# Folding the first four tiles' rows four items earlier, in the last group of the down stage

## The chip, the cores and the metric

The kernel runs on one core of a Trainium2 chip. The time is device microseconds (us) of one execution, the median of several. The core has five engines: TensorE (PE in the profile, its weight loads PEld), VectorE (DVE), ScalarE (ACT), GpSimd (POOL), and SyncE (SP), which here only issues DMAs. ACT can issue DMAs as well, and the kernel uses that in one place.

## The reference, cut to what matters

There are 2 x 1024 = 2048 rows of width 1024. A first part with a sparse gate is followed by a layernorm, then a feed-forward network with 2-rank LoRA terms and a second layernorm.

```
s = silu(x @ w_gate.T)                       # 2752 wide
s[the k = 1376 smallest of |s| in each row] = 0
s = s * (x @ w_up.T)
x = layernorm(x + s @ w_down.T)

def qlora(x, wq, A, B):                      # A: 2 x d, B: h x 2
    return x @ tile(wq, (1, 4)).T + (x @ A.T @ B.T) * 0.5
gate = silu(qlora(x, w1q, a1, b1))
up = qlora(x, w3q, a3, b3)
x = layernorm(x + qlora(gate * up, w2q, a2, b2))
```

`tile(wq, (1, 4))` repeats a weight of width 256 four times, so `x @ tile(wq).T` equals the sum of the four 256-wide quarters of a row times `wq`. The kernel calls that sum the fold. The products `x @ A.T` are four dot products of length 1024 for each row (two of a1, two of a3).

## The kernel before, in words

The rows are cut into 16 tiles of 128 and these into 4 groups of GT = 4 tiles. All matrix products use fp32 values split into two parts of a shorter form, high and low (names ending in h and l), so that each product is done in three passes: high by high, high by low, low by high. The stages follow each other: gate and up for all groups, the selection of the largest values (DVE and ACT), then `down` for the groups 0 to 3, then `ffn` for the groups 0 to 3.

**`down(g)`** has six blocks of the 2752-wide inner dimension (512, 512, 512, 384, 384, 448) times the 4 tiles of the group: 24 items. An item loads its values m and its mask u on SP's queue (L710, L711), makes the mask a number on ACT (L724), multiplies on POOL (L725), transposes on PE (L745, L747) into PSUM, copies the high part on ACT (L749) and the low part on DVE (L750), then multiplies with the weights on PE (L765), and DVE adds the result to `acc` (L768). After the last block of a tile follow its layernorm (L568 and on, with a power on POOL in L580 and an application on ACT in L588) and a store of the row tile to `x_d` in DRAM (L787). Weights for a block come either from a stored split (L684) or raw (L603), and then ACT makes the high part (L173) and POOL the low part (L174).

**The last group of down** does the beginning of the ffn beside its items. From the fifth item on, `ffn_consts` is advanced by one step for each item: four loads of the rows of a1 and a3 to all partitions, `abc` (L798), and then for each of 8 blocks of the hidden width the matrix `br` of the LoRA factors b1 and b3: a memset (L806), six small loads (L810), a split on ACT and POOL (L173, L174), and two DMAs on ACT's queue (L813). Their staging buffers `braw` have two copies. From the item on at which the block number is `f1` = 2, `f1_first` is advanced by one step for each item. For t = 0 to 3 it loads tile 8 + t (L656), makes the four dot products of that tile on DVE (L659), then the fold and the LoRA factors of tile t (`f1_tile`), and, one step later, their transposes (`f1_tile2`).

**`f1_tile(t)`** loads the tile of x (`x2a`, L920, 512 KB), adds the quarters in three operations on POOL (L927, L928, L929) into `fold`, and lays the four dot products out in `tl` (a memset on POOL, L933, and small operations on DVE, L931 to L940). **`f1_tile2(t)`** does four transposes on PE (L949, L951), a copy of the high part on ACT (L954) and of the low part on DVE (L955). The dot products of the tiles 0 to 7 are made earlier in `down`. `fold` and `tl` have one buffer each, `x2a` two, and `fh` and `fl`, the copies' results, six. In `f1_first` the dot products' throwaway output also goes to the buffer `fold` of that step.

**`ffn(g)`** has 8 blocks x 4 tiles: 14 matmuls each (L981 to L984), a silu on ACT (L987), and products on DVE (L988, L990), with further work on ACT (L992) and POOL (L994). Beside the blocks 0, 2, 4 and 6 it makes the folds of the next group's tiles (tiles 4 to 7 in group 0), by the same two functions. After that come `f2` and the second layernorm.

**The order.** The order of the instructions of each engine is fixed when the kernel is built, by a scheduler which plans with its own model of time from the order in which the program issues them. SP's DMA queue is in program order as the scheduler left it.

Of the kernel before, what the change touches and what calls it, by code (L numbers as in the profile page):

```python
# [32 lines left out]
GT = 4  # L33
# [19 lines left out]
class Ring:  # L53
    def __init__(self, n, slots, dt):
        self.n, self.slots, self.dt = n, slots, dt
# [10 lines left out]
class Kern:  # L66
    def __init__(self, tc, A, O):
        self.tc, self.nc, self.A, self.O = tc, tc.nc, A, O
        self.nt = A["xt"].shape[0]
        self.x_seen = False  # L70
        self.lasta = self.lastv = self.lastd = None
        self.pend = self.lastp = None
        self.cache, self.wd_d, self.wd_g, self.wst = {}, {}, {}, []

# [533 lines left out]
    def down(self, g, f1=None, early=0):  # L608
        n, ea = 0, []
        for ib in range(len(DB)):  # L610
            if f1 is not None:
                if ib == f1:
                    self.fg = self.f1_first()
            ws = []
            for t in range(g * GT, (g + 1) * GT):
                st = {"e": n} if n < early else {}
                load = lambda: self.down_load(st, ib, t, n)
                prep = lambda st=st, ib=ib: self.down_prep(st, ib)
                mm = lambda st=st, ib=ib, t=t, ws=ws: self.down_mm(st, ib, t, ws)
                if n < early:  # L620
                    load()
                    ea.append((self.pend, prep))
                    self.q2.append(mm)
                    if n == early - 1:
                        for j in range(2):
                            yield
                            with self.behind():
                                for e in ea:
                                    e[j]()
                        self.pend = None  # L630
                        yield
                else:
                    self.masks()
                    self.item(lambda: (load(), self.down_w(g, ib, ws)), prep, mm, 2, 3)
                n += 1
                if g == 0 and n == 12:
                    self.tkg = self.topk(self.nt // GT - 1, 2)
                if (n > 11 or g) and self.tkg and next(self.tkg, 1):
                    self.tkg, self.dg = None, self.dots_down()
                if f1 is not None and n > 4:  # L640
                    next(self.fcg, None)
                    if ib >= f1:
                        next(self.fg, None)
                for _ in range(2 if n % 2 else 1):
                    next(self.dg, None)
        if f1 is not None:
            list(self.fg)
            self.masks()
        yield

    def f1_first(self):
        for t in range(GT):
            f, x2 = self.f1_room()
            jk, o = f.bitcast(U8), t + 2 * GT
            with self.load_behind():
                self.nc.sync.dma_start(x2, self.x_d[o])  # L656
            for i in range(4):
                with self.behind():
                    self.nc.vector.scalar_tensor_tensor(  # L659
                        jk, x2, 0.5, self.abc[:, i, :], ALU.mult, ALU.mult, accum_out=self.dall[:, o, i : i + 1]  # L660
                    )
                if i < 3:
                    yield
            self.f1_tile(t, f)
            yield
            self.f1_tile2(t)

    def f1_room(self):
        return (self.fp.tile([P, w], F, tag=n, bufs=b, name=n) for n, w, b in (("fold", 2 * P, 1), ("x2a", H, 2)))
# [119 lines left out]
    def ffn_consts(self):  # L789
        nc, fp = self.nc, self.fp  # L790
        A = self.A
        self.br = fp.tile([P, NI], R, name="br")
        self.abc = fp.tile([P, 4, H], F, name="abc")
        self.fst, self.c2 = {}, False
        for i in range(4):
            yield
            with self.load_behind():
                nc.sync.dma_start(  # L798
                    self.abc[:, i, :], A[("a1", "a3")[i // 2]][i % 2 : i % 2 + 1, :].partition_broadcast(P)
                )  # L800
        for b in range(NB):
            yield
            bs = slice(b * BW, (b + 1) * BW)
            sv = fp.tile([P, 2, BW], F, tag="sv", bufs=2, name="braw")
            raw, lo = sv[:, 0], sv[:, 1].bitcast(R)
            nc.gpsimd.memset(raw, 0.0)  # L806
            with self.load_behind():
                for w, n in ((0, "b1t"), (32, "b3t")):
                    for i in range(3):
                        nc.sync.dma_start(raw[w + 2 * i : w + 2 * i + 2, :], A[n][:, bs])  # L810
            self.split(self.br[:, bs], lo, raw)
            for w in (0, 32):
                nc.scalar.dma_start(self.br[w + 2 : w + 4, bs].bitcast(F), lo[w + 2 : w + 4, :].bitcast(F))  # L813
# [278 lines left out]
```

## Time and profile before

| quantity | value |
|---|---|
| median of 3 runs | 1924.16 us (1921.65 to 1924.33) |
| the profiled execution | 1926.91 us |
| its span | 1925.1 us |
| mean granted TensorE clock | 0.993 |
| PE busy | 1885.3 us, 98% of the span |
| DVE, ACT, POOL busy | 64%, 47%, 51% |
| DMA, mean over the span | 254 GB/s |

The page's rows of groups give, for each line and engine, the operation, its buffers and shapes, how often it ran, its busy time and mean, and the idle time just before it with what ended it. In the timeline each row is the start in us from the span's start, the busy time, the engine and line, the operation and, in square brackets, the idle time before and its releaser. A duration of a PE row overlaps with the next row's start, so the pace is read from one start to the next. The last group of down lies, on PE, at about 1330 to 1475 us; the first blocks of ffn follow.

### The profile page before, as it was taken

Reading aid. Unit: us, or ns where it says so; the run is one execution under the profiler, and the core shown is the slowest. Engines: PE = TensorE matmul, PEld = TensorE weight load, DVE = VectorE, ACT = ScalarE, POOL = GpSimd, SP = SyncE. Lnnn points to the kernel's source line nnn. Section 1 sums busy time; section 2 is a strip of 40 time slices with the busy share of each in tenths; the row PEclk is TensorE's granted clock in tenths of the full one; section 3 lists DMA queues with packets and bytes.
Section 4 is the critical chain, followed back from the end, with each engine's and each line's share of the span. In section 5 each row is a group of like instructions: output and inputs, shape, how many; then the busy total and the mean of one; then the engine's idle time right before and its main releaser. Section 6 shows DMA issues by size and latency. Waiting matters only on the chain. (4 is left out here: it accounts for less than half of the span.)

```text
span 1925.1 us, 29381 instructions
## 1 busy us (share of the span) xinstructions
PE 1885.3 (98%) x10825; PEld 1754.4 (91%) x10825; DVE 1229.6 (64%) x1831; ACT 904.0 (47%) x1448; POOL 973.0 (51%) x606
## 2 busy tenths in 40 slices
PE   9999999999999999999999999999998999998998
PEld 9999999999999999999888787888787979898896
DVE  4633556767358574691238998688467857779565
ACT  4333477414883258622246533323333746557362
POOL 5655664445445354355565443554565746436062
PEclk9999999999999999999999999999999999999999
DMA  7677687676977868667798756977776878485651
GB/s 266 237 250 260 236 325 261 210 272 253 330 231 241 314 235 303 236 228 256 282 328 285 270 188 227 337 245 261 268 250 244 279 284 321 155 318 177 229 196 66
DMA packets 166205, 488.66 MB, mean 254 GB/s; under 512 B 24772, under 2 KB 45380, under 8 KB 166056
## 3 DMA queue, kind: packets, MB, share of 16 engines
q1 hardware_dynamic: 165848, 486.43, 71.9%
q8 instruction: 85, 1.39, 0.3%
q14 instruction: 64, 0.52, 0.1%
q10 hardware_dynamic: 208, 0.31, 0.0%
HBM read 370.30 MB, written 116.33 MB: 253 GB/s over the span
## 5 line engine op out<-in xcount | busy, mean ns | idle before, releaser
L174 POOL TENSOR_TENSOR wl<-wr,wh 128x1376 fp32r<-128x1376 f32 (+2 forms) x187 | 566.4, 3035 | 466.1 <-ACT wh L173 436.8
L353 PE MATMUL mm<-wh,xh 128*128 128x344 f32 x1928 | 610.4, 322 | 2.8 <-DMA wh<-tw3T1h 2.8
L353 PE MATMUL mm<-wh,xl 128*128 128x344 f32 x1928 | 609.8, 320 | 0.0
L173 ACT CAST wh<-wr 128x1376 fp32r<-128x1376 f32 (+2 forms) x192 | 232.4, 1215 | 340.9 <-PE mm L353 199.6
L353 PEld LDWEIGHTS mm<-wh,xh 128*128 128x128 f32 x1928 | 364.7, 189 | 3.0 <-issue 3.0
L353 PEld LDWEIGHTS mm<-wh,xl 128*128 128x128 f32 x1928 | 364.6, 189 | 0.0
L353 PE MATMUL mm<-wl,xh 128*128 128x344 f32 x1928 | 342.1, 319 | 0.0
L353 PEld LDWEIGHTS mm<-wl,xh 128*128 128x128 f32 x1928 | 310.1, 188 | 0.0
L765 PE MATMUL mm<-wh,mh 128*128 128x512 f32 x680 | 217.8, 400 | 0.1
L765 PE MATMUL mm<-wl,mh 128*128 128x512 f32 x680 | 215.1, 395 | 1.1 <-POOL wl L174 1.1
L765 PE MATMUL mm<-wh,ml 128*128 128x512 f32 x648 | 205.5, 396 | 0.8 <-DVE ml L750 0.8
L460 ACT ACTIVATE jk<-a,cur 128x2752 int8<-128x2752 f32 x66 | 170.8, 2588 | 31.2 <-DVE cur L482 15.8
L994 POOL TENSOR_TENSOR hf<-hf,gt 128x344 f32<-128x344 f32 x96 | 142.2, 1491 | 75.6 <-DVE gt L988 68.7
L725 POOL TENSOR_TENSOR m<-m,ub 128x512 f32<-128x512 f32 (+2 forms) x93 | 111.0, 1194 | 128.0 <-ACT ub L724 65.8
L981 PE MATMUL mm<-wh,fh 128*128 128x344 f32 x512 | 166.2, 325 | 5.8 <-DVE gt L988 5.2
L983 PE MATMUL mm<-wh,fl 128*128 128x344 f32 x512 | 164.0, 320 | 0.0
L982 PE MATMUL mm<-wl,fh 128*128 128x344 f32 x512 | 163.9, 320 | 0.0
L765 PEld LDWEIGHTS mm<-wl,mh 128*128 128x128 f32 x680 | 127.4, 188 | 30.1 <-POOL wl L174 2.2
L768 DVE TENSOR_TENSOR acc<-acc,mm 128x1024 f32<-128x1024 f32 x96 | 116.4, 1214 | 57.9 <-PE mm L765 27.8
L765 PEld LDWEIGHTS mm<-wh,mh 128*128 128x128 f32 x680 | 124.7, 189 | 24.8 <-ACT mh L749 0.5
L765 PEld LDWEIGHTS mm<-wh,ml 128*128 128x128 f32 x648 | 121.2, 189 | 26.9 <-DVE ml L750 1.0
L992 ACT ACTIVATE pa<-pa 128x344 f32<-128x344 f32 x256 | 123.0, 483 | 38.6 <-DVE pa L990 34.0
(191 smaller groups left out, 2742.5 us busy)
## 6 DMA issues: line engine op xcount, KB each, us to landing
wr<-wu SPq DMA_DIRECT2D x64, 688.0 KB
wr<-wg SPq DMA_DIRECT2D x52, 688.0 KB
wr<-wd SPq DMA_DIRECT2D x48, 512.0 KB
s_d<-cc SPq DMA_DIRECT2D x64, 344.0 KB
m_d<-mt SPq DMA_DIRECT2D x64, 344.0 KB
a<-s_d SPq DMA_DIRECT2D x64, 344.0 KB
wl<-wc_w SPq DMA_DIRECT2D x48, 344.0 KB
wh<-wc_w SPq DMA_DIRECT2D x48, 344.0 KB
```

The costliest lines, as they stand in the source:

```text
L173: self.lasta = self.nc.scalar.copy(hi, raw)
L174: (eng or self.nc.gpsimd).tensor_tensor(lo, raw, hi.bitcast(F), ALU.subtract)
L353: self.nc.tensor.matmul(o, l, r, start=start and n < m and n % (2 * KH) == 0, stop=stop and n >= m and (n - m) % KH == KH - 1)
L460: nc.scalar.activation(jk.bitcast(I8), av[j], AF.Sign, bias=t, scale=-1.0, accum_out=s)
L725: nc.gpsimd.tensor_tensor(m[:, :w], m[:, :w], ub[:, :w], ALU.mult)
L765: nc.tensor.matmul(ps[:, h], a, b[:, h * 512 : (h + 1) * 512], start=i == 0, stop=i == len(ops) - 1)
L768: nc.vector.tensor_tensor(out, out, ps.rearrange("p a b -> p (a b)"), ALU.add)
L981: nc.tensor.matmul(o, fh[:, c, :], wh[:, c, :], start=c == 0, stop=False)
L982: nc.tensor.matmul(o, fh[:, c, :], wl[:, c, :], start=False, stop=False)
L983: nc.tensor.matmul(o, fl[:, c, :], wh[:, c, :], start=False, stop=False)
L992: nc.scalar.activation(pa[:, r], pa[:, r], AF.Copy, scale=0.5, accum_out=part[:, r, b : b + 1])
L994: G.tensor_tensor(hf[:, hs], hf[:, hs], gt, ALU.add)
```

## The change

The first tile's fold, `f1_tile(0)`, is called once when block `f1` − 1 = 1 begins, ahead of `f1_first`. In `f1_first`, step t now begins with the transposes of tile t (`f1_tile2(t)`), then loads tile 8 + t and makes its dot products, and then calls `f1_tile(t + 1)`, the fold of the next tile. So tile 0's fold is made eight items sooner, those of tiles 1 to 3 and all four tiles' transposes four items sooner. Two assignments move to the constructor. The number of instructions on each engine does not change.

```diff
@@ __init__
         self.lasta = self.lastv = self.lastd = None
+        self.fst, self.c2 = {}, False
...
@@ down
             if f1 is not None:
+                if ib == f1 - 1:
+                    self.f1_tile(0)
                 if ib == f1:
                     self.fg = self.f1_first()
...
@@ f1_first
         for t in range(GT):
+            self.f1_tile2(t)
             f, x2 = self.f1_room()
...
                 if i < 3:
                     yield
-            self.f1_tile(t, f)
-            yield
-            self.f1_tile2(t)
+            if t < GT - 1:
+                self.f1_tile(t + 1, f)
+                yield
...
@@ ffn_consts
         self.abc = fp.tile([P, 4, H], F, name="abc")
-        self.fst, self.c2 = {}, False
```

## The prediction

> **What bounds the kernel now.** I read the page's first part, then the waits of PE in the stretch that the change touches (1330 to 1560 us of the span), then PE's timeline there.
>
> ```profile
> PE 1885.3 (98%) x10825; PEld 1754.4 (91%) x10825; DVE 1229.6 (64%) x1831; ACT 904.0 (47%) x1448; POOL 973.0 (51%) x606
> ```
>
> PE is the bound nearly everywhere. The change leaves every engine's instruction count alone, so it can only move PE's waits and the slow-clock stretches behind them. The waits of PE by releaser (total us, times, longest):
>
> ```profile
> PE tp L949 <- POOL fold L929: 3.2, 2, 1.9
> ...
> PE tp L745 <- POOL m L725: 1.6, 1, 1.6
> ...
> PE tp L745 <- DVE fl L955: 1.2, 1, 1.2
> PE mm L765 <- POOL wl L174: 1.1, 3, 0.5
> PE mm L765 <- DVE ml L750: 0.8, 1, 0.8
> PE mm L981 <- DVE hf L988: 0.5, 1, 0.5
> PE tp L951 <- DVE tl L940: 0.4, 1, 0.4
> ```
>
> These sum to 8.8 us (the L1028 and three L988 rows lie after 1525 us and are not touched). PE's timeline places them:
>
> ```profile
> 1376.14 0.66 PE L745 MATMUL tp<-ident,m 128*128 128x128 f32 x4 [1.62 <-POOL m L725]
> ...
> 1381.59 0.44 PE L949 MATMUL tp<-ident,fold 128*128 128x128 f32 x2 [1.35 <-POOL fold L929]
> ...
> 1457.91 0.55 PE L745 MATMUL tp<-ident,m 128*128 128x128 f32 x3 [1.17 <-DVE fl L955]
> ...
> 1477.96 0.44 PE L949 MATMUL tp<-ident,fold 128*128 128x128 f32 x2
> 1478.78 0.41 PE L951 MATMUL tp<-ident,tl 128*128 128x128 f32 x2 [0.38 <-DVE tl L940]
> 1481.06 0.44 PE L949 MATMUL tp<-ident,fold 128*128 128x128 f32 x2 [1.87 <-POOL fold L929]
> ```
>
> Two of the places also cost clock. In the windows (length, PE busy, granted clock, DMA share, GB/s):
>
> ```profile
> 1461.00:1463.00 2.00, 2.00 (x6) 0.56 0.77 295
> 1479.00:1481.00 2.00, 0.19 (x2) 1.00 0.91 264
> 1483.00:1485.00 2.00, 2.00 (x9) 0.56 0.96 391
> ```
>
> Behind 1459.3 eight down matmuls take 3.5 us where they take 1.84 at full clock (.461 a pair): 1.7 lost. Behind 1483.2 twelve of the ffn take .287 each instead of .157: 1.5 lost. The waits at 1376 and 1381 lose none. The whole reachable loss is 8.8 + 1.7 + 1.5 = 12.0 us, against a profiled execution of 1926.91 (span 1925.1, 1.8 around it), itself 2.75 above the median of 1924.16. No gain can pass 12 us; I apply differences to the median.
>
> **The change part by part.** F0 to F7 are the transposes L949/L951 of tiles 0 to 7, T1 to T96 the item transposes L745. In the built order PE has 2,080 down matmuls L765. Before, F0 to F4 stand after 1752, 1848, 1944, 2026 and 2058 of them; after, F0 to F3 after 1656, 1778, 1854 and 1960.
>
> 1. Tile 0's fold, eight items sooner. The L920 load (512 KB) goes on SP's queue right behind a store L787 at about 1330 (before: 1351.4), ahead of the next k_d and abc loads, each pushed by one issue, .3 to .7 us. A load of that kind issued at 1349.2 landed at 1357.7 with the DMA share at 1.03; at 1330 the share is .99, so 5 to 8 us, landing 1335 to 1338. The fold is three POOL operations at .74 to 1.37 (2.5 in the 1478 row), now ahead of the last layernorm's L580 and one mask L725. Of the next item's prep, the first need, PE has some 3 us in hand; if the load lands after 1338, each us costs one. I take 0, bounds 0 and 3. F0 at about 1354 finds its fold some ten us old: the 1.35 wait goes. Gain 1.35.
>
> 2. T82's wait of 1.62. Its cause is ACT:
> ```profile
> 1372.26 0.59 ACT L749 CAST mh<-tp 128x512 fp32r<-128x512 f32 x1 [6.39 <-DMA br<-braw]
> ```
> The L813 pair on ACT's queue holds ACT for 6.4 us, so the mask cast L724 and L725 are late. After, 20 down matmuls (4.6 us) more stand ahead of T82, but POOL has tile 1's fold (2.5) ahead of that mask. 4.6 − 2.5 leaves 2.1 against a wait of 1.62. Gain 1.6, bounds 0 and 1.6. F1 has then 26 more matmuls behind T82's place to wait in; its fold is about 3 us ahead. No wait.
>
> 3. F3 and the item behind it. Before, F3's copy L954 stands behind two casts that wait for a weight load:
> ```profile
> 1453.09 1.44 ACT L173 CAST wh<-wr 128x688 fp32r<-128x688 f32 x2 [7.76 <-DMA wr<-w]
> 1454.43 0.58 ACT L954 CAST fh<-tp 128x512 fp32r<-128x512 f32 x1
> ```
> fl, T94 and the next ml follow late: 1.17 + .77, and 1.7 of half clock. After, F3 stands 66 matmuls (15 us) earlier and its copy behind only the first cast; T94 and T95 have 75 straight matmuls behind them. Gain 3.6, bounds 1.5 (the cast still late) and 3.6.
>
> 4. New ACT order. The casts L724 of items 17 and 18 (before at 1402.1 and 1407.9) and F2's copy now stand behind an L813 pair that waits for its split; T88, T89, T90 and F3 hang on them. The row nearest is again an L813 hold, 6.39 here and 5.78 at 1418; against it stand 3 to 4 us by which masks and copies run ahead of PE. If the pair issues with the gap of the single row (.57 to 2.3), it costs nothing; with one full hold 2 to 3; with both more (rival B). I take 1.0, between, nearer the small end since only one braw of two is still in flight.
>
> 5. Weight splits L174 on POOL. Folds stand ahead of two of them: 2.5 us of delay for a wl that now is .27 to .5 late in three places (1.1 in all). Bounds 0.4 and 4; I take 1.5, so 0.4 worse.
>
> 6. F4 to F7. Before, F4 stands at the end of down, F5 after 2 blocks of ffn work (14 matmuls each, 2.2 us), F6 and F7 side by side after 3: the .38 and 1.87 waits and the 1.5 of clock. Cause: there is one fold buffer, and the next fold starts only when its reader is done. L949 to L949 is 3.1 us (1477.96 to 1481.06). After, F4 and F5 stand side by side after 3 blocks, F6 after 6, F7 after 10. So the pair still exists, for other tiles: wait 3.1 − .44 = 2.7, in place of .38 + 1.87 + .51 = 2.8. F6 and F7 lie 6.6 and 8.8 us apart: none. Gain .1 on the wait.
>
> Does F5's wait cost clock? The row says 2.8 us of waits with transposes between lost 1.5. The Trainium skill, TensorE: Matmul & The Clock Gate, Part 1 (The HAM clock gate), says the half rate comes after at least one idle window of about 3.4 us in a free-running window; by that a 2.7 us wait alone would cost none, and the forecast would be 1.5 lower. But Part 4 (PE-mode transpose) says transposes do not count as PE-busy in the same way; with F4's and F5's transposes around it the stretch without counted work is 3.6 us, and the rule then agrees with the row. The row: 1.5, no gain.
>
> 7. Further on the order is the same and a shift carries through. POOL's folds of tiles 6 and 7 go later into a stretch where POOL is 17.5 of 20 us busy (1500 to 1520): 0, bounds 0 and 2.
>
> Nothing is subtracted from PE's work: F0 to F7 each cost the same .45.
>
> Sum of gains: 1.35 + 1.6 + 3.6 − 1.0 − .4 + .1 = 5.2; less .4 for a wl or ml late by one more copy (the four prep copies that change places with folds on ACT and DVE, .4 to .6 each, one of them uncovered): 4.9. Profiled 1926.9 → 1922.0; median 1924.16 → **1919.3**.
>
> **Rivals.** A, *only moved* (1923.5): the wait for the mask goes to T88, the splits lose 2 more us and the F4/F5 pair replaces F6/F7. Then 1.35 + 1.6 + 3.6 = 6.5 is met by 4 in step 4 and 2 in step 5: 0.6 faster. For it: every queue here runs within 4 us of PE. Against: T88 to F3 are four places, and a delay is paid once, not at each.
>
> B, *slower* (1928.3): the ACT queue. If both holds (6.39 and 5.78, 12.2 together) recur just ahead of the casts of items 17 and 18, the masks come 12.2 − 3.8 = 8.4 late at T88; PE stops and loses 1.6 of clock: 10.0, less the 5.9 otherwise gained (4.9 + the 1.0 charged): 4.1 slower. It decides the sign once ACT is 8.1 us behind where it ran: 3.8 in hand, and 5.9 of gain less 1.6 of clock. For it: the L813 holds in the trace are that long. Against: an issue on ACT's queue waits for the POOL split and a load, and these stand no later than before.
>
> C, *the load of tile 0 lands late* at 1330, in the fullest stretch of DMA (1 us for each us after 1338): at 1342 it takes 4, leaving 1923.2; counted with A.
>
> **How the numbers follow.** Forecast .43, A with C .27, B .30. Measurement can tell about 0.2% (3.85 us) from nothing. Forecast's own range 1914.5 to 1920.3: the far end of gains is 12.0 less F5's 2.7 (and, if the rule holds, none of its clock), so 9.3 faster, 1914.8. A fills 1920.3 to 1926, B 1926 to 1934; range **1914.5 to 1930**, leaving out the worse half of B. Faster .43, same .27, slower .30.
>
> **What would show it.** Right: no wait at F0 and none at F3/T94, no half clock between 1380 and 1470; two L949 side by side with a wait of 2.7 on POOL L929 and half clock behind it; PE's waits from 1330 to 1500 at some 5 us. Wrong: a wait of over 3 us at T88 to T90 released by L725 with ACT idle on br<-braw (B); waits on L174 above 1.5 (A); an L749 late by over 2 us near 1340 with the x2a load landing after 1338 (C). The forecast is wrong too if PE's half clock appears where a wait is shorter than 2 us.

## The result, and the profile after

The changed kernel is slower: 1926.64 us against 1922.28 us (medians of 22 runs each), a ratio of 1.0025 with a 95% interval of 1.0017 to 1.0033. That is 4.4 us more where 4.9 us less was forecast. The profiled execution took 1926.05 us (span 1924.3), so the two profiles suggest the opposite of the medians: the one of before, at 1926.91, lies 4.6 us above its kernel's median, the one of after 0.6 below. The traces are therefore read for the place and the cause of single losses, and the sizes are taken from medians.

In the changed kernel the line numbers are 1 to 4 higher: L745 is L749, L765 is L769, L724 and L725 are L728 and L729, L813 is L816, L949 is L952, L929 is L932, L981 is L984, L988 is L991, L994 is L997. In some of the experiments they are a few higher still, so there the tile names are the better guide. The first view is the waits of PE of the changed kernel, in the same stretch, 1330 to 1560 us, which was shown for before (us in total, times, longest).

```profile
PE mm L984 <- DVE gt L991: 6.2, 5, 2.4
PE tp L749 <- POOL m L729: 3.7, 1, 3.7
PE mm L769 <- ACT hh L1031: 2.8, 1, 2.8
PE tp L952 <- POOL fold L932: 2.3, 1, 2.3
PE mm L769 <- ACT mh L753: 0.9, 1, 0.9
PE tp L749 <- POOL cm L172: 0.5, 1, 0.5
```

Gone are the waits that the prediction wanted gone: F0's for its fold, those for the weight splits, and the stall at F3 (fl and ml). What is there instead is one long wait for a mask, and waits in the ffn for L991 that grew from 1.6 to 6.2 us. The row of before, which the prediction's view left out, is

```profile
PE mm L981 <- DVE gt L988: 1.6, 3, 1.0
```

PE's timeline of the changed kernel puts them in place.

```profile
1370.76 1.11 PE L749 MATMUL tp<-ident,m 128*128 128x128 f32 x4 [3.71 <-POOL m L729]
...
1475.53 0.69 PE L952 MATMUL tp<-ident,fold 128*128 128x128 f32 x2 [2.35 <-POOL fold L932]
1501.86 0.42 PE L984 MATMUL mm<-wh,fh 128*128 128x344 f32 x1 [1.41 <-DVE gt L991]
1517.72 0.42 PE L984 MATMUL mm<-wh,fh 128*128 128x344 f32 x1 [2.42 <-DVE gt L991]
1535.22 0.42 PE L984 MATMUL mm<-wh,fh 128*128 128x344 f32 x1 [1.57 <-DVE gt L991]
```

The wait at 1370.76 also costs clock. The windows of PE there (length, PE busy, granted clock, DMA share, GB/s):

```profile
1370.00:1372.00 2.00, 1.24 (x5) 0.50 0.50 131
1372.00:1374.00 2.00, 2.00 (x6) 0.50 0.41 103
1374.00:1376.00 2.00, 2.00 (x7) 0.50 0.06 14
```

Counting PE's work at its usual pace from one transpose to the next (.2305 us for a down matmul, .09 for a transpose), the place at 1370.76 lost 4.0 us and the stretch behind it 2.6, together 6.6. This is T81, the item transposes just before T82. ACT's timeline of the changed kernel shows why its mask was late:

```profile
1358.52 0.62 ACT L728 CAST ub<-u 128x512 bf16<-128x512 uint8 x1
1367.02 1.79 ACTq L816 DMA_DIRECT2D br<-braw  x2
1368.86 0.62 ACT L728 CAST ub<-u 128x512 bf16<-128x512 uint8 x1 [9.72 <-DMA br<-braw]
```

The first pair of `br` DMAs stood on ACT's queue from 1359 to 1368.8. POOL had made its source by 1359.6 (L175 on braw started at 1358.70 and took .93), so the pair did not wait for data. It waited for semaphores. The trace keeps, for each instruction, the semaphores that it waits for and the times at which they were raised. In this stretch SP's DMAs use eight of them in turn, each raised when its DMA lands. The two DMAs of the pair wait for two that were in use by loads of the second `braw`, in this row of SP's timeline:

```profile
1360.10 0.91 SPq L813 DMA_DIRECT2D braw<-b1t  x3
```

These are the second and the third of the row, which SP issued at 1360.44 and 1360.74. From 1360 to 1366 the DMA share was 0.93 to 1.03, and they landed at 1366.95 and 1367.14. The pair began at 1367.02. Before, it was the same with other loads: the pair's two DMAs began at 1366.88 and 1370.25, within .1 us of the landing of two weight loads (1366.81 and 1370.23) on the same semaphores. ACT's timeline of before shows which cast stood where:

```profile
1364.76 0.62 ACT L724 CAST ub<-u 128x512 bf16<-128x512 uint8 x1 [0.29 <-DMA u<-k_d]
...
1366.88 5.28 ACTq L813 DMA_DIRECT2D br<-braw  x3
...
1374.23 0.62 ACT L724 CAST ub<-u 128x512 bf16<-128x512 uint8 x1
```

The mask cast of T81 stood ahead of the pair and that of T82 behind it (T82's wait of 1.62). Now T81's stands behind it.

The ffn's loss is read from POOL's timeline of the changed kernel:

```profile
1496.32 1.58 POOL L997 TENSOR_TENSOR hf<-hf,gt 128x344 f32<-128x344 f32 x1
1497.86 1.37 POOL L930 TENSOR_TENSOR fold<-x2a 128x256 f32<-128x256 f32 x1
1499.17 0.20 POOL L936 MEMSET tl<- 128x134 f32 x1
1499.34 0.93 POOL L997 TENSOR_TENSOR hf<-hf,gt 128x344 f32<-128x344 f32 x1
1500.23 0.73 POOL L931 TENSOR_TENSOR fold<-fold,x2a 128x256 f32<-128x256 f32 x1
1501.89 1.62 POOL L997 TENSOR_TENSOR hf<-hf,gt 128x344 f32<-128x344 f32 x1 [0.93 <-DVE gt L991]
1503.47 1.37 POOL L932 TENSOR_TENSOR fold<-fold,x2a 128x256 f32<-128x256 f32 x1
```

A fold is mixed into the L997 additions. It is that of tile 8, the first tile of the group after next, so the ninth fold, made as soon as the one `fold` buffer is free. POOL's timeline of before has it at 1482 to 1486, ahead of the first L994:

```profile
1482.28 0.73 POOL L927 TENSOR_TENSOR fold<-x2a 128x256 f32<-128x256 f32 x1 [0.29 <-DMA x2a<-x_d]
1483.09 1.25 POOL L928 TENSOR_TENSOR fold<-fold,x2a 128x256 f32<-128x256 f32 x1
1484.42 1.31 POOL L929 TENSOR_TENSOR fold<-fold,x2a 128x256 f32<-128x256 f32 x1
...
1499.10 1.62 POOL L994 TENSOR_TENSOR hf<-hf,gt 128x344 f32<-128x344 f32 x1 [2.02 <-DVE gt L988]
```

Now F7, which frees the buffer, comes after 10 blocks in place of 3, and the ninth fold lands where POOL has no room. DVE shows the other half:

```profile
1499.41 0.89 DVE L941 COPY tl<-dr 128x2 f32<-128x2 f32 x1 [0.78 <-POOL tl L936]
...
1501.30 0.51 DVE L991 TENSOR_TENSOR gt<-gt,mm 128x344 f32<-128x344 f32 x1
```

DVE's copies for `tl` wait for a POOL memset that is queued behind the fold, and the product L991, for which PE waits at 1501.86, is behind them.

### The profile page after: what moved, and what is told of

The parts are those of the page before. It is cut to its first block, busy times and chain, and to the rows that moved or that the text cites. A ratio compares the mean times of both kernels' runs of the same rounds, so it can differ in the third digit from the quotient of the medians.

```text
span 1924.3 us, 29371 instructions
## 1 busy us (share of the span) xinstructions
PE 1884.4 (98%) x10825; PEld 1757.4 (91%) x10825; DVE 1227.3 (64%) x1831; ACT 904.5 (47%) x1448; POOL 974.7 (51%) x606
## 5 line engine op out<-in xcount | busy, mean ns | idle before, releaser
L175 POOL TENSOR_TENSOR wl<-wr,wh 128x1376 fp32r<-128x1376 f32 (+2 forms) x187 | 568.6, 3047 | 469.4 <-ACT wh L174 442.5
L769 PE MATMUL mm<-wh,mh 128*128 128x512 f32 x680 | 218.5, 401 | 0.9 <-ACT mh L753 0.9
L769 PE MATMUL mm<-wl,mh 128*128 128x512 f32 x680 | 215.2, 395 | 0.0
L769 PE MATMUL mm<-wh,ml 128*128 128x512 f32 x648 | 206.2, 396 | 0.0
L997 POOL TENSOR_TENSOR hf<-hf,gt 128x344 f32<-128x344 f32 x96 | 140.4, 1471 | 74.6 <-DVE gt L991 67.7
L729 POOL TENSOR_TENSOR m<-m,ub 128x512 f32<-128x512 f32 (+2 forms) x93 | 110.8, 1191 | 127.3 <-ACT ub L728 74.5
L984 PE MATMUL mm<-wh,fh 128*128 128x344 f32 x512 | 166.6, 326 | 8.8 <-DVE gt L991 8.8
L769 PEld LDWEIGHTS mm<-wl,mh 128*128 128x128 f32 x680 | 127.8, 189 | 28.0
L769 PEld LDWEIGHTS mm<-wh,mh 128*128 128x128 f32 x680 | 125.1, 189 | 25.7 <-ACT mh L753 1.3
L769 PEld LDWEIGHTS mm<-wh,ml 128*128 128x128 f32 x648 | 121.2, 189 | 25.9
```

What stands on the lines that cost most here:

```text
L175: (eng or self.nc.gpsimd).tensor_tensor(lo, raw, hi.bitcast(F), ALU.subtract)
L729: nc.gpsimd.tensor_tensor(m[:, :w], m[:, :w], ub[:, :w], ALU.mult)
L769: nc.tensor.matmul(ps[:, h], a, b[:, h * 512 : (h + 1) * 512], start=i == 0, stop=i == len(ops) - 1)
L984: nc.tensor.matmul(o, fh[:, c, :], wh[:, c, :], start=c == 0, stop=False)
L997: G.tensor_tensor(hf[:, hs], hf[:, hs], gt, ALU.add)
```

## The experiments

Each run was compared with runs of the kernel before on the same chip. Differences are of medians, in us against that before. The ratio was not formed from the two medians, and the two measures differ by up to 1.3 us (2.1 in the row of e1_early): the sizes below are known no better than that. The last two columns are of the one profiled execution. A stretch is taken from the same transpose (1555 down matmuls into the program) to the first matmul of f2. The first column is what it lost by PE's pace up to the end of down, the second is the time of the stretch less that loss. The diffs are shortened, and their comments are added here.

```
kernel              diff   ratio [95%]               loss in down   rest
before                -    -                             11.9      214.0
changed             +4.4   1.0025 [1.0017, 1.0033]       10.0      217.1
e1_early            +9.6   1.0061 [1.0044, 1.0077]       16.9      214.2
e2_pair_late        +5.3   1.0027 [1.0016, 1.0038]       10.6      217.9
e3_pin_tile7        +5.1   1.0033 [1.0020, 1.0046]        9.0      216.9
e4_shift            +5.9   1.0032 [1.0019, 1.0045]       13.0      217.6
e5_pair0            +3.0   1.0016 [1.0008, 1.0025]        9.1      217.1
e6_tail             +7.0   1.0036 [1.0022, 1.0051]       15.2      215.1
e7_pair0_tail       +3.4   1.0015 [1.0007, 1.0024]       12.0      215.8
e8_hold_only        +1.1   1.0005 [0.9997, 1.0014]       10.8      213.2
e9_pin8             +1.0   1.0010 [1.0003, 1.0017]        9.0      213.4
e10_pair0_pin8      -1.4   0.9997 [0.9987, 1.0006]        7.3      214.3
e11_before_pin8     -0.5   0.9996 [0.9982, 1.0010]        9.7      212.1
e12_dve567          -0.9   0.9997 [0.9986, 1.0007]        8.0      213.0
```

The expectations keep the line numbers of the kernel before. They start from two theories: H, that the hold on ACT costs, and T, that the ffn does. A rival E is that the early load of tile 0 costs.

**Tile 0's fold alone sooner.**

```diff
 in f1_first, beside the early f1_tile(0):
-            self.f1_tile2(t)
             f, x2 = self.f1_room()
...
-            if t < GT - 1:
-                self.f1_tile(t + 1, f)
-                yield
+            if t:
+                self.f1_tile(t, f)
+            yield
+            self.f1_tile2(t)
```

> Only tile 0's fold is made sooner; tiles 1 to 3 and all transposes keep the order of before. The first DMA pair of br on ACT then stands ahead of the mask cast of the ninth item, as in the changed kernel, while the folds of tiles 4 to 7 stand as before. Theory H (that hold costs a wait of some 3.7 us and 3 us of clock, in all nearly 7, against 3 us of waits gone): 3 to 5 us slower than before, one L745 wait of over 3 us released by POOL's mask. Theory T (the loss is in the ffn, from the late fold of tile 7): within 1 us of before or faster, because its tail is that of before.

It was slower by 9.6, twice the most that H expected. The hold was there, as expected, but this order kept all that the rest of the change takes away, and made it worse. PE's timeline of this run:

```profile
1368.97 0.66 PE L749 MATMUL tp<-ident,m 128*128 128x128 f32 x4 [3.92 <-POOL m L729]
1431.53 0.44 PE L952 MATMUL tp<-ident,fold 128*128 128x128 f32 x2 [1.19 <-POOL fold L932]
...
1460.46 0.90 PE L749 MATMUL tp<-ident,m 128*128 128x128 f32 x3 [2.40 <-DVE fl L958]
```

So H's hold exists, and the shift of the other tiles, which goes with it in the changed kernel, is worth several us in down.

**Tile 0's fold four items later again.**

```diff
-                if ib == f1 - 1:
+                if ib == f1:
                     self.f1_tile(0)
```

> The changed kernel with tile 0's fold called four items later, at the start of block 2. Rival E (the early load of tile 0 in the fullest stretch of DMA is what costs): as fast as before. Theories H and T: as slow as the changed kernel, 3 to 6 us above before, since the scheduler still puts the load and the fold in nearly the same places (two DMA issues later).

As slow as the changed kernel (+5.9 and +4.4, with intervals that overlap), and with the same wait, 5.08 here. The scheduler puts the load two DMA issues later, one addition of its fold behind a mask, and nearly all the rest where the changed kernel has it. The block at which tile 0 is called thus matters little: the scheduler moves it up anyhow. This falls against rival E in the form in which the call's place is what costs. A load held back to its place of before was not tried, but the run with both costs moved, further down, keeps the early load and is no slower than before.

**All pairs behind the next mask cast.**

```diff
+            yield
+            with self.tc.issue_after(self.lastm.ins):        # lastm: the last L724
                 for w in (0, 32):
                     nc.scalar.dma_start(...)
```

> The changed kernel, with each pair of br DMAs issued one item later and behind that item's mask cast on ACT. Theory H: the 3.7 us wait and the half clock after it go, 5 to 7 us faster than the changed kernel, so about 1 to 3 us faster than before. Theory T: no more than 1 us faster than the changed kernel, still 3 to 5 us slower than before, since the folds of tiles 6 and 7 stand where the changed kernel has them.

This kernel leaves out the last of the eight pairs, and so the low part of the LoRA factors of the last block. The T81 wait was gone, but the time did not fall (+5.3): F3 now waited 4.65 for its fold on POOL. (The next expectation calls it F2; it is the fourth fold of the trace, that of tile 3.) Moving eight pairs moved too much, so the next run moves one.

**The first pair alone behind the mask cast.** The edit is that of the run before, with `if b == 0`. Its `yield` does more than the expectation says: all later steps of `ffn_consts` come one item later too.

> The changed kernel with only the first pair of br DMAs put behind the next mask cast on ACT; the order of the ffn's folds stays that of the changed kernel. Theory H (the hold of the mask costs some 6.5 us in the changed kernel): the 3.7 us wait and the half clock behind it are gone, 1 to 3 us faster than before, unless another wait takes the place, as F2's for its fold did when all pairs were moved; then as slow as the changed kernel. Theory T (the loss lies in the ffn): 3 to 5 us slower than before, as the changed kernel.

1.4 us faster than the changed kernel (+3.0 against +4.4), not 5 to 7. PE's timeline of this run in the stretch:

```profile
1388.34 0.73 PE L769 MATMUL mm<-wl,mh 128*128 128x512 f32 x2 [0.56 <-POOL wl L175]
1391.80 0.73 PE L769 MATMUL mm<-wl,mh 128*128 128x512 f32 x2 [0.68 <-POOL wl L175]
1440.56 0.55 PE L749 MATMUL tp<-ident,m 128*128 128x128 f32 x3 [1.01 <-DVE fl L961]
1451.33 0.52 PE L749 MATMUL tp<-ident,m 128*128 128x128 f32 x3 [1.98 <-DVE ml L754]
```

The wait for the mask is gone, all 3.7 us and its half clock. But four waits, 4.2 in all, stand where the changed kernel has two, 1.4 in all, behind T81, and the one at 1451 has half clock behind it (0.50 in the next window). A kernel in which a stall of 6.6 us is gone is only 1.4 faster, and the intervals of the two ratios still overlap. Why is open. PE may meet the other engines sooner, where they are still late. But the order from T81 to the end of down changed as well, through that `yield`: SP's later loads of `braw` stand elsewhere between the other loads, and F3 stands 12 down matmuls sooner. No run moves the pair and nothing else.

**The hold alone, put into the kernel before.**

```diff
+        with self.tc.issue_after(self.pair0.ins):            # first br pair
             nc.scalar.copy(ub[:, :w], u[:, :w])
```

> The kernel before, with the mask cast of the item behind the first pair of br DMAs pinned behind that pair on ACT; the transposes F0 to F7 keep their places within some 10 matmuls. Theory H: an L745 wait of 3 to 5 us for POOL's mask and half clock behind it, 4 to 7 us slower than before. If the hold is only long under the changed kernel's DMA order (rival E, the early load): no more than 1.5 us slower.

Not told from before (+1.1, interval across 1). The cast stands behind the pair, but the pair was held less (L815 and L725 are L813 and L724 here):

```profile
1362.51 1.80 ACTq L815 DMA_DIRECT2D br<-braw  x2
1364.36 0.62 ACT L725 CAST ub<-u 128x512 bf16<-128x512 uint8 x1 [3.93 <-DMA br<-braw]
```

3.9 us of hold in place of 9.7, and .80 of wait on PE. The trace shows why. The first DMA of the pair shares its semaphore with a weight load here, which SP issued at 1358.64, ahead of two more weight loads, and it began at 1362.51, just behind that load's landing at 1362.44. The second began at 1363.74, just behind the landing of the next weight load at 1363.72. Standing behind the pair is thus not enough. In all three traces the hold lasts until the loads that share its semaphores have landed, and these are others here. This pin, too, changed the order of the rest of down (two waits for fl, 1.89 and 2.42, each with half clock behind it), so +1.1 isn't the price of a hold of 3.9 us alone.

**The fold of tile 7 held back, in the kernel before.**

```diff
+        with self.tc.issue_after(self.pin7.ins):             # first tile's L994 of block 2
             self.f1_tile(tiles[-1] + 1 + b // 2)             # for g == 0, b == 6
```

> The kernel before, with the fold of tile 7 held back on POOL until after the first L994 of block 2, and F7 so after 15 blocks of the ffn instead of 3; nothing else moves. Theory T: DVE's copies for tl wait for POOL in the middle of the products, L981 waits for L988 rise from 1.6 to some 5 us, and against it the 2.8 us of waits and 1.5 us of clock at F7 go: about the same to 2 us slower than before. Theory H: nothing to do with it, so the time falls by the 4 us that go at F7, or by less.

+5.1, more than T expected, with the order of down untouched (a loss of 9.0 in its trace). The pin also drove the fold of tile 8, which needs the same buffer, into the L994 additions. This was the first sign that the ffn can pay for the whole of the loss.

**The folds of tiles 4 to 7 sooner, in the changed kernel.**

```diff
-                    if b:
+                    if b and g:
                         self.f1_tile2(tiles[-1] + b // 2)
                     self.f1_tile(tiles[-1] + 1 + b // 2)
+                    if not g:
+                        self.f1_tile2(tiles[-1] + 1 + b // 2)
```

> The changed kernel with the order of down untouched, and each of the folds of tiles 4 to 7 asked for with its transposes in one step, so that POOL has done all four before the first L994 of the ffn. Theory T: the waits for L988 in the ffn fall from 6 us to under 2, 3 to 5 us faster than the changed kernel, within 1.5 us of before. Theory H alone: the 3.7 us wait and its half clock stay, and nothing else matters, so 4 to 5 us slower than before.

No gain (+7.0). The waits in the ffn did fall, and the rest with them, from 217.1 to 215.1. But F4 now stands at 2027 down matmuls, where F3 stood before, and meets the same stall that F3 had been moved away from:

```profile
1460.04 0.55 PE L749 MATMUL tp<-ident,m 128*128 128x128 f32 x3 [1.16 <-DVE fl L960]
1461.47 0.73 PE L769 MATMUL mm<-wh,ml 128*128 128x512 f32 x2 [0.77 <-DVE ml L754]
```

With the first pair moved as well:

> Both edits of the two runs ahead of it. If H and T are two separate costs, their gains add: 8 to 11 us faster than the changed kernel, so 4 to 6 us faster than before. If a hold or a late fold only moves elsewhere: within 2 us of before.

+3.4: the same stall at F4 (1.15 and .78), so nothing is settled by these two but that a fold set at that place pays for it, whichever tile it is.

**The ninth fold alone.** After these runs the theory T was put anew: the ffn's loss is the fold of tile 8.

```diff
+        with self.tc.issue_after(self.lastg.ins):            # last L994 of the first ffn group
             self.f1_tile(tiles[-1] + 1 + b // 2)             # for g == 1, b == 0
```

> The changed kernel with one thing moved: the fold of tile 8, the first of the next group, is held back on POOL until the last L994 of the first ffn group (in the changed kernel it falls among the first of them). Theory T in its new form (the changed kernel's loss is that ninth fold, which lands in the stretch where POOL is full; the losses counted by anchors put 3.6 us there): the waits for L988 at the second and third block fall from 3.8 to under 1 us, 3 to 4 us faster than the changed kernel, 0 to 1.5 us slower than before. If POOL is late there without it: no more than 1 us faster than the changed kernel.

The expectation calls tile 8 the next group's; it is the first of group 2, asked for in the ffn of group 1. PE's order is that of the changed kernel, and on POOL nothing else moved. On ACT and DVE one weight split near 1521 changed its place, and on SP the loads behind tile 8's own (1505 in the changed kernel) moved up. +1.0 against +4.4: 3.4 us of the 4.4. The waits of PE from 1330 to 1546:

```profile
PE tp L749 <- POOL m L729: 3.6, 1, 3.6
PE mm L985 <- DVE gt L992: 2.8, 5, 1.4
PE tp L953 <- POOL fold L933: 2.3, 1, 2.3
PE tp L749 <- DVE ml L754: 1.5, 2, 0.8
```

The waits for the product fell from 6.2 to 2.8. The hold at T81 is still there, as in all five traces in which the first pair was left where the changed kernel has it (3.3 to 5.1 us of wait). In this one execution F5's wait happens to cost no clock, which the pin does not touch, so the size is taken from the medians and not from the trace.

**Both.**

> The changed kernel with the first br pair behind the mask cast and the fold of tile 8 held back. The costs of hold and ninth fold add (theories H and T): 1.4 + 3.5 us faster than the changed kernel, so 0.5 to 1.5 us faster than before. If the fifth fold's own wait and clock, which neither edit touches, is what is left: still 1 us slower than before.

−1.4, with an interval across 1: the two together take away the whole loss. Beside the run with the first pair alone, PE's order is the same and only the ninth fold moved, as in the run before: 4.4 us faster (+3.0 to −1.4), with intervals that do not meet. So the ninth fold is measured twice, at 3.4 and 4.4 us (2.9 and 3.7 by the ratios). The edit of the first pair, with all that its `yield` moves, comes to 1.4 without the pin and 2.4 with it.

**The same pin in the kernel before.**

> The kernel before with the fold of tile 8 held back to the same place. Before, that fold runs at 1482 to 1486, ahead of the first L994, so holding it back should do little: within 1 us of before (a gain of up to 1 for the work it takes from DVE and POOL there). If it gains 3 us or more, then the pin is good for another reason than the one of theory T.

No difference that can be told. The pin is worth something only where the ninth fold stood badly.

**The fifth fold's wait.** The same as both, and in `f1_tile` of the tiles 5, 6 and 7 the additions and the memset on DVE:

```diff
+        G = V if t in (5, 6, 7) else G
```

> As the last but one, and the three additions of the folds of tiles 5, 6 and 7 and their memset on DVE in place of POOL. The changed kernel's fifth fold waits 2.35 us for POOL, with some 2 us of half clock behind it; on DVE three additions of 128x256 take near 1 us in place of 2.4. Theory T: that wait falls by 1 to 1.5 us and the clock loss with it, 2 to 3 us faster than the run without it, so 2.5 to 4 us faster than before. If DVE is as full there as POOL, the products L988 behind it come late: no faster.

Not faster than the run without it: the fold wait fell from 2.33 to 1.77, and a wait of .81 for the first product came behind it. DVE is busy for 5.4 of the 6 us from 1470 on there, where POOL was for 5.0 in the run without the edit. Beside before it is the same, so no version was found that beats both kernels.

## Why the prediction was wrong, by its steps

**Step 1** (tile 0's fold, gain 1.35, load at 1330 no loss) held: F0 waits for nothing, and no copy was late near 1340.

**Step 2** (T82, gain 1.6, bounds 0 and 1.6) failed. T82's wait is gone, but the step looked at T82 alone. What stands behind the first `br` pair changed with the order, and T81's mask now does. It lost 4.0 us and some 2.6 more of slow clock in the trace; taking the pair away from there gave 1.4 to 2.4 us back. Rival B had the mechanism, a mask cast behind an ACT hold, but looked for it at T88 to T90 behind later pairs, and **step 4** charged 1.0 for it there. At T88 to T90 PE waited for nothing. The bound excluded a loss that the row beside it (6.39 us of hold) could have given. What rival B held against itself, that an issue on ACT's queue waits for POOL's split and a load that stand no later than before, was the wrong wait: the pair waited for the landing of other loads of SP, 7.4 us after its source was ready. Rival B's sum, 4.1 slower, lies next to the measured 4.4, but by luck, since most of the loss came from the ffn.

**Step 3** (F3 and its neighbours, 3.6) held in kind: no stall and no half clock there, with 1.4 us of smaller waits at its place. The run with F4 in F3's old place shows that this stall is one of the place.

**Step 5** had the wrong sign: 0.4 worse was taken, and the split waits of 1.1 went in the profiled execution. That they went because PE stood for 6.6 us ahead of them is likely, not shown. With the first pair moved, two of them came back.

**Step 6** held: F4 and F5 side by side, a wait of 2.35 where 2.7 was forecast, with half clock behind it (0.50 in the window at 1476). The wait is there in every trace with these folds on POOL and in this order (2.33 to 2.35); but it cost clock in only three of those six traces, so the half clock that was forecast is there by luck.

**Step 7** (nothing, bounds 0 and 2) is the largest miss: 3.4 and 4.4 us by the two runs that move the ninth fold alone. It named the folds of tiles 6 and 7, and took POOL's idle 2.5 of 20 us for room. It missed that F7's shift from 3 to 10 blocks also delays the next user of the same buffer, tile 8, and put no price on DVE's queue, in which a copy that waits for POOL holds the products that PE needs.

**The base.** The profiled waits were applied in full to the median. T82's wait of 1.62 is not in the traces of the two experiments that have the front order of before (their losses in down are 9.0 and 9.7, not 11.9), so up to some 2 us of the gain was never there to be had. Nor was the clock: the 1.7 us of half clock at T94 are in before and in the second of these traces but not in the first, though the waits of 1.0 to 1.2 and of .8 us are in all three, and the 1.5 behind F7's wait of 1.87 are missing in the second, which has that wait.

Put together: moving the two costs away gains 5.8 us against the changed kernel and ends at before's time. Why it does not end below it is open. In the traces, down then loses 7.3 in place of 9.7 in the kernel before with the same pin, and the rest is 2.2 longer (214.3 and 212.1), mostly by half clock behind F5's wait of 2.33 where none follows F6's and F7's waits of 2.26 in the other. But that is one execution of each.

## What to carry to other kernels

Moving work earlier moves the next users of its buffers too: follow a single-buffered tile to the next two or three tiles beyond those that the edit names, and ask on which engine they land. For an engine's queue with a DMA issue in it, list what stands behind that issue in the new order, from the nearest item on, and price each at the full hold seen in the profile. Ask also whose semaphores that DMA shares: its source can be ready long before it may start. A wait taken off an engine that is 98% busy can be worth much less than its length (a stall of 6.6 us went here and the time fell by 1.4), and an edit that moves one thing in a program can move many in the built order: compare the two orders before the time is put down to the one thing.

## What the runs showed of the hardware that was not expected

The same wait cost clock in one run and none in another. In the changed kernel F5 waited 2.35 us and the window behind it ran at 0.50; with tile 8 held back F5 waited 2.34, between the same transposes, and the windows behind it, up to 1546, were at 1.00 (first row the changed kernel, second row the other).

```profile
1476.00:1478.00 2.00, 2.00 (x10) 0.50 1.02 285
1476.00:1478.00 2.00, 2.00 (x14) 1.00 0.78 244
```

Of the waits in the ffn, 2.42 at 1517.72 left the clock alone in the changed kernel, and 2.63 at the same place was followed by 0.50 in the run with the first pair moved. The length does not order them either: 2.12 at 1515.57 in the run with tile 7 held back, with no transposes near it, was followed by 0.56, while 2.95 at 1522.43 in the run with all pairs moved was followed by 1.00. So neither the idle window nor the count of transposes with which step 6 reasons decides it here, and the prediction's flat 1.5 us behind such a wait was one draw.

A DMA issued by ACT stood for 7.4 us after its source was ready; the landing of other DMAs with the same semaphores set that time, 9.7 us of hold in one order and 3.9 in another.
